# Strassen projections in 49 block products: two sets of PSUM banks, and x, bv and the result summed at the output by accumulating DMAs

## The chip, the core and the metric

The kernel runs on one NeuronCore of one Trainium2 chip. A core has TensorE (PE, with its weight loads as PEld), VectorE (DVE), ScalarE (ACT), GpSimd (POOL) and SyncE (SP), which here only issues DMAs; 16 DMA engines serve their queues. Each engine works through its own instructions in order and waits on semaphores for the others. The metric is device time in microseconds. Times are those of single executions and their median; the profile is of one more execution.

## What is computed

The input x has 128 batches of 128 rows (nodes) by 512 columns. All is float32. Cut to what matters:

```
h  = relu(layernorm(x))                       # layer 0
A  = adj @ h                                  # 128 x 512 per batch
x1 = x + relu(max_n A + b0)                   # one number c per row of each batch
h  = relu(layernorm(x1)); q, k, v = h @ Wq + bq, h @ Wk + bk, h @ Wv + bv
w  = softmax(q k^T / 8 + mask(adj))           # 8 heads of 64 columns
out = x1 + w v
```

The kernel uses that adding c to a whole row changes nothing in the layernorm after it (but for eps), so one normalised h serves both layers; and that the mask can be a product with 0 or 1 after the exponential. bv is added to the end result, since the weights sum to 1. Sums of weights that leave a safe range would send the program to a plain second path (`general`), which does not run with these inputs.

## The kernel before, in words

Batches are taken in 32 groups of four (G = 4); a group is processed in a pipeline, while the projections of q and k are made for the next group and the normalisation for the one after it. The three projections are matrix products of 512 x 512 (4 batches x 128 rows against 512 columns, over 512), done by the Strassen-Winograd scheme: the operands are cut into halves in both directions, and seven products of halves, p1 to p7, take the place of eight. A second level cuts five of the seven (p2, p3, p4, p5, p7) once more into seven products of quarters, each one 128x128x128 matmul, while p1 and p6 stay as four matmuls of 256 columns. So a projection has 8 matmuls of 256 columns (L483) and 35 of 128 (L596). In the first group (q, k and v) and for the last group's v the five are not cut.

The operands of such products are sums. `h_sum` (L381) makes sums of halves of the transposed h (t1 to t4), `h_blocks` (L398, on POOL) the sums of quarters; `weight_sums` and `weight_blocks` do the same for the weights, once, at the start. The products are combined in PSUM where signs allow, and else outside: terms that enter several results are kept in scratch banks, and DVE adds them to U, T7 and the results (L648, L674, L527, L536), POOL adds T7 to U (L699), ACT copies with the bias (L498). PSUM has eight banks of 512 columns; a bank that is written again must have been read before.

In each group, in PE's order: `apply` of the group before (64 matmuls L795; DVE divides by the sums, L812 and L813), `scores` (32 matmuls, L765; ACT exponentiates, L773), then v of this group, q and k of the next. In between stand one matmul for the adjacency of a batch (`product`, L350; DVE takes its maximum, L354), the layernorm (DVE L286 and L287, ACT L300 and L301, POOL's small operations, `norm_end` on ACT, L310), and the transpose of h: DVE transposes 32x32 blocks (`blocks`, L323), and 16 DMAs of SP put them in place (`move`, L333). POOL multiplies the weights by the mask (L777), adds bv to x (L316) and x to the result (L825); ACT adds c to x (L821); SP stores one batch at a time (L826).

The order is written out by hand (`manual_schedule`): each engine has its instructions in the order in which the Python code issues them, with no scheduler. `steps`, `later` and the table `next_norms` say after which product which other work is issued. Tiles come from pools with a set number of buffers: x has 7 (pairs of batches), most sums have one.

Of the kernel before, what the change touches and what calls it, by code (L numbers as in the profile page):

```python
# [52 lines left out]
P = 128  # L53
G = 4
# [115 lines left out]
def tile_adj_preln_d2(  # L170
# [16 lines left out]
    T = G * D  # L187
    HT2 = T // 2

# [3 lines left out]
    WS = {n: const.tile([P, 4, 2, N // 2], F32, name=f"s{n}_sb") for n in "qkv"}  # L193

    WB = {
        n: const.tile([P, 4 if n == "v" else 3, 4, P], F32, name=f"ss{n}_sb") for n in "qkv"
    }
# [5 lines left out]
    mhalf = const.tile([P, 1], F32, name="mhalf")  # L203
# [3 lines left out]
    db_sb = const.tile([P, 2, 2], F32, name="db_sb")  # L207
    DB = {n: db_sb[:, i] for i, n in enumerate("qk")}
    ones = const.tile([P, 1], F32, name="ones")
    flag = const.tile([1, 1], I32, name="flag")  # L210
    V = const.tile([P, G, H, HE], F32, name="v")
    U = const.tile([P, 3, 2, N // 2], F32, name="u")
    T7 = const.tile([P, 2, N // 2], F32, name="t7")

    def fast(ctx):
        xpool = ctx.enter_context(tc.tile_pool(name="xpool", bufs=7))
# [7 lines left out]
        X, HN, TB, HT, HB, H2, QT, KT, C, AMAX, WA, RSTD, NMR, PR = ({} for _ in range(14))  # L224
# [26 lines left out]
        nc.scalar.activation(live[:, 0:1], mhalf, AF.Copy)  # L251
# [7 lines left out]
        for p in range(2, 5):  # L259
            load(p)  # L260
# [3 lines left out]
        nc.gpsimd.memset(V[:, :, :, HD:HE], 1.0)  # L264
# [6 lines left out]
        def norm(m):  # L271

            g, i = divmod(m, G)
            if i == 0:
                HT[g] = proj.tile([P, G, NC, D], F32, name="hT")
                AMAX[g] = stat.tile([P, G], F32, name="amax")
                C[g] = stat.tile([P, G], F32, name="c")
            if m < G:
                if m == 0:
                    O[0] = one.tile([P, G, N], F32, name="o")  # L280
                HN[m] = O[0][:, m]
            else:
                HN[m] = work.tile([P, N], F32, name="hn", bufs=3)
            st = stat.tile([P, 6], F32, name="st")
            mv = stat.tile([P, 2], F32, name="mv")
            nc.vector.bn_stats(st, x_of(m))  # L286
            nc.vector.bn_aggr(mv, st)  # L287
            ve = stat.tile([P, 1], F32, name="ve")
            nc.vector.tensor_scalar_add(ve, mv[:, 1:2], EPS)
            rstd = RSTD[m] = stat.tile([P, 1], F32, name="rstd")  # L290
            nc.gpsimd.tensor_tensor(rstd, ve, mhalf, op=ALU.pow)
            nmr = NMR[m] = stat.tile([P, 1], F32, name="nmr")
            nc.gpsimd.tensor_scalar(nmr, mv[:, 0:1], rstd, -1.0, op0=ALU.mult, op1=ALU.mult)

        def norm_act(m):

            HN[m] = work.tile([P, N], F32, name="hn", bufs=3)
            neg = stat.tile([P, 1], F32, name="neg", bufs=2)
            sq = stat.tile([P, 1], F32, name="sq", bufs=2)
            nc.scalar.activation(HN[m], x_of(m), AF.Copy, scale=-1.0 / N, accum_out=neg)  # L300
            nc.scalar.activation(HN[m], x_of(m), AF.Square, bias=neg, accum_out=sq)  # L301
            ve = stat.tile([P, 1], F32, name="ve")
            nc.gpsimd.tensor_scalar(ve, sq, 1.0 / N, EPS, op0=ALU.mult, op1=ALU.add)
            rstd = RSTD[m] = stat.tile([P, 1], F32, name="rstd")
            nc.gpsimd.tensor_tensor(rstd, ve, mhalf, op=ALU.pow)
            nmr = NMR[m] = stat.tile([P, 1], F32, name="nmr")
            nc.gpsimd.tensor_tensor(nmr, neg, rstd, op=ALU.mult)  # L307

        def norm_end(m, bv=True):
            nc.scalar.activation(HN[m], x_of(m), AF.Relu, scale=RSTD[m], bias=NMR[m])  # L310
            if m >= G and bv:
                add_bv(m)

        def add_bv(m):
            x_m = x_of(m)
            nc.gpsimd.tensor_tensor(x_m, x_m, bv_sb, op=ALU.add)  # L316
# [28 lines left out]
        PA = {}  # L345

        def product(m):

            PA[m] = bank(7 if m >= G else 5 + m % 2)
            nc.tensor.matmul(PA[m], adjT, HN[m], start=True, stop=True)  # L350

# [10 lines left out]
        def h_quarters(g):  # L362
            if g in HB:
                return
            t = HT[g]

            t1 = t[:, 2:4, 0:2]
            if g == 0:
                t1 = one.tile([P, 4, D], F32, name="h23").rearrange("p (t c) d -> p t c d", t=2)
            HB[g] = dict(  # L370
                t1=t1,
                b11=t[:, 0:2, 0:2], b12=t[:, 2:4, 0:2], b21=t[:, 0:2, 2:4], b22=t[:, 2:4, 2:4]
            )

        def h_sum(g, k, eng=nc.vector):

            o, a, b = ("t3 b22 b12", "t1 b12 b11", "t2 b22 t1", "t4 b21 t2")[k].split()
            h_quarters(g)
            if o != "t1":
                HB[g][o] = one.tile([P, 2, 2, D], F32, name=f"hs{k}")  # L380
            eng.tensor_tensor(HB[g][o], HB[g][a], HB[g][b], op=ALU.subtract)  # L381

        def h_blocks(g, k, parts=range(3)):

            h_quarters(g)
            b = HB[g]["t4 b22 b21 t1 t3".split()[k]].rearrange("p t c d -> p c t d")
            if 0 in parts:
                H2[g, k] = one.tile([P, 4, D], F32, name=f"h2{k}")
            t = H2[g, k]

            sums = (
                (t[:, 0:2], b[:, :, 1], b[:, 0]),
                (t[:, 2], b[:, 1, 1], t[:, 0]),
                (t[:, 3], b[:, 1, 0], t[:, 2]),
            )
            for i in parts:
                o, x, y = sums[i]
                nc.gpsimd.tensor_tensor(o, x, y, op=ALU.subtract)  # L398

        def w_blocks(n, k):  # L400

            if k < 3:
                return [WB[n][:, k, e] for e in range(4)]
            if k == 3:
                a = WA[n]["a21"]
                return [a[:, e // 2, e % 2 * P : (e % 2 + 1) * P] for e in range(4)]
            if n == "v":
                return [WB[n][:, 3, e] for e in range(4)]
            return [WA[n][a][:, 0, P : 2 * P] for a in "a22 s4 a12 s1".split()]

        def weight_blocks(eng, n, ks=(3, 2, 0, 1, 4)):

            for k in ks:
                a = WA[n]["a22 s4 a12 s1 s3".split()[k]].rearrange("p c (o f) -> p o c f", o=2)
                s = w_blocks(n, k)
                for o, x, op, y in (
                    (s[0], a[:, 1, 0], ALU.add, a[:, 1, 1]),
                    (s[2], s[0], ALU.subtract, a[:, 0, 0]),  # L420
                    (s[1], a[:, 0, 0], ALU.subtract, a[:, 1, 0]),
                    (s[3], a[:, 0, 1], ALU.subtract, s[2]),
                ):
                    eng.tensor_tensor(o, x, y, op=op)

        def weight_sum(eng, n, k):

            if k == 0:
                w = W[n]
                WA[n] = dict(  # L430
                    a11=w[:, 0:2, 0:HT2], a21=w[:, 0:2, HT2:N],
                    a12=w[:, 2:4, 0:HT2], a22=w[:, 2:4, HT2:N],
                    **{f"s{j + 1}": WS[n][:, j] for j in range(4)},
                )
            o, a, op, b = ("s1 a21 + a22", "s2 s1 - a11", "s3 a11 - a21", "s4 a12 - s2")[k].split()
            eng.tensor_tensor(  # L436
                WA[n][o], WA[n][a], WA[n][b], op=ALU.add if op == "+" else ALU.subtract
            )
# [5 lines left out]
        class Products:  # L444

            def __init__(self, g, n):
                self.g, self.n = g, n
                self.run, self.five = {}, {}
                self.k0 = 3 if n == "q" else 0
                if n == "q":
                    QT[g] = one.tile([P, NC, T], F32, name="qT")
                elif n == "k":
                    KT[g] = one.tile([P, NC, T], F32, name="kT")  # L460
                o_t = "(o d) -> p {} o t d" if n == "v" else "(t d) -> p {} o t d"
                r = "t" if n == "v" else "o"
                self.bk = lambda x: x.rearrange(f"p {r} " + o_t.format(""), d=D)

            def dst(self, f, t):

                if self.n == "v":
                    return V[:, 2 * t : 2 * t + 2, 4 * f : 4 * f + 4, 0:HD]
                o = (QT if self.n == "q" else KT)[self.g]
                return o[:, 2 * f : 2 * f + 2, t * HT2 : (t + 1) * HT2]  # L470

            def view(self, ap):
                return ap.rearrange("p r (h d) -> p r h d", d=HD) if self.n == "v" else ap

            def mm(self, bank, a, b, first=False, parts=range(4)):
                a, b = WA[self.n][a], HB[self.g][b]
                for i in parts:
                    r, c = divmod(i, 2)
                    if self.n == "v":
                        lhs, rhs = b[:, r, c], a[:, c]  # L480
                    else:
# [552 lines left out]
```

## Time and profile before

| what | value |
|---|---|
| median of 3 runs | 1491.02 us (1489.36 to 1491.72) |
| span of the profiled execution | 1491.1 us |
| granted TensorE clock, mean | 0.998 |
| time from a group's scores to the next one's | 45.66 us |
| matmul records | 14565 |
| DMA share of 16 engines | 27.3% on SP's queue, 105.66 MB in all |
| POOL's queue for DMAs | 176 packets, 0.27 MB (four small loads at the start) |

The profiled execution's own time is its span: from the first to the last instruction it is 1491.1 us, and the median of the runs is the same within 0.1 us. How to read the lines that follow: in a timeline the first number is the start in us from the span's start, the second the length; then engine, source line, operation, output and inputs by name, output shape, how many instructions are merged. In brackets stands the engine's idle time just before, and what ended it. Each float32 matmul leaves two records in the trace, so counts of PE records are about twice those of matmuls. Lengths of instructions that follow each other overlap by some hundredths of a microsecond, so the cost to an engine is better read from start to start.

### The profile page before, as it was taken

The numbers are of one execution on the slowest core, as the hardware profiler recorded it, in microseconds if no ns is written. First come the engines' busy times: TensorE is split into PE (matmuls) and PEld (weight loads), VectorE is DVE, ScalarE is ACT, GpSimd is POOL, SyncE is SP. The second block draws the span as 40 slices with busy tenths as digits, with TensorE's granted clock in tenths as the row PEclk, the third lists the DMA queues.
The fourth block names the chain that finished last, engine by engine and source line by source line (L and its number), as shares of the span: only waits on it lengthen the run. The fifth ranks groups of instructions, "written<-read, shape, count | busy, mean of one in ns | idle before, by whom it ended". The sixth has DMA issues, their size and how long they took to land.

```text
span 1491.1 us, 38559 instructions
## 1 busy us (share of the span) xinstructions
PE 1467.8 (98%) x14565; PEld 1336.0 (90%) x14565; DVE 1170.0 (78%) x2909; ACT 680.0 (46%) x1550; POOL 1326.0 (89%) x1578
## 2 busy tenths in 40 slices
PE   8999999999999999999999999999999999999997
PEld 6899989999999999899999999999999989999997
DVE  7787877778877778777787777787777877778877
ACT  3444454454454444544544544445444444444442
POOL 7989989899899898898998989989999989899882
PEclk9999999999999999999999999999999999999999
DMA  4232222331223322233222233122332222331211
GB/s 167 55 86 52 54 77 77 86 74 38 77 75 83 86 41 65 76 78 86 60 52 74 76 85 86 29 76 76 79 86 55 54 75 76 86 86 26 63 43 59
DMA packets 307835, 105.66 MB, mean 71 GB/s; under 512 B 273152, under 2 KB 273280, under 8 KB 307648
## 3 DMA queue, kind: packets, MB, share of 16 engines
q1 hardware_dynamic: 307328, 102.84, 27.3%
q8 instruction: 117, 1.92, 0.5%
q14 instruction: 70, 0.57, 0.1%
q0 software_dynamic: 176, 0.27, 0.1%
q10 hardware_dynamic: 144, 0.07, 0.0%
HBM read 37.03 MB, written 33.55 MB: 47 GB/s over the span
## 4 chain that ended last, share of the span: by engine, by line
PE 67%; POOL 26%; DVE 3%; SPq 1%; issue 1%; DMA 1%; ACT 0%; DVEq 0%; POOLq 0%
PE bk L596 30%; POOL h L398 17%; PE bk L483 16%; PE bk L795 8%; PE bk L765 8%; POOL u L699 7%; PE bk L350 5%; POOL hs L381 2%; SPq L333 1%; DVE u L674 1%; DMA wk_sb<-in_L_gnn_Wk_dram 1%; DVE hs L381 0%; DVE sk_sb L436 0%; DMA hT<-tb 0%; DVE o L813 0%
## 5 line engine op out<-in xcount | busy, mean ns | idle before, releaser
L777 POOL TENSOR_TENSOR w<-w,live 128x512 f32<-128x512 f32 x248 | 308.5, 1277 | 0.0
L699 POOL TENSOR_TENSOR u<-u,t 128x512 f32<-128x512 f32 x184 | 235.0, 1277 | 74.1 <-DVE t L648 50.2
L674 DVE TENSOR_TENSOR u<-u,bk 128x256 f32<-128x256 f32 x552 | 206.3, 414 | 65.1 <-POOL u L699 39.0
L773 ACT ACTIVATE w<-bk 128x512 f32<-128x512 f32 x256 | 128.9, 624 | 270.4 <-PE bk L765 270.4
L648 DVE TENSOR_TENSOR u<-u,bk 128x128 f32<-128x128 f32 x368 | 109.2, 317 | 101.3 <-PE bk L596 99.4
L825 POOL TENSOR_TENSOR o<-xp,o 128x512 f32<-128x512 f32 x122 | 152.1, 1283 | 20.1 <-DVE RS L812 20.1
L310 ACT ACTIVATE hn<-xp,nmr,rstd 128x512 f32<-128x512 f32 x124 | 100.7, 812 | 142.9 <-POOL nmr L307 98.1
L316 POOL TENSOR_TENSOR xp<-xp,bv_sb 128x512 f32<-128x512 f32 x128 | 159.2, 1276 | 0.7 <-issue 0.7
L354 DVE TENSOR_REDUCE amax<-bk 128x1 f32<-128x512 f32 x128 | 86.6, 677 | 79.1 <-PE bk L350 79.1
L795 PE MATMUL bk<-v,w 128*64 128x65 f32 x4096 | 128.5, 223 | 0.0
L795 PEld LDWEIGHTS bk<-v,w 128*64 128x64 f32 x4096 | 124.0, 138 | 4.1 <-issue 0.3
L350 PE MATMUL bk<-hn,adjT 128*128 128x512 f32 x248 | 126.9, 593 | 0.0
L498 ACT ACTIVATE u<-bk,bq_sb 128x256 f32<-128x256 f32 x124 | 52.6, 480 | 160.2 <-PE bk L483 160.2
L765 PE MATMUL bk<-qT,kT 64*128 64x128 f32 x2048 | 122.9, 275 | 0.0
L765 PEld LDWEIGHTS bk<-qT,kT 64*128 64x128 f32 x2048 | 116.8, 188 | 2.5 <-issue 0.3
L596 PE MATMUL bk<-ssv_sb,h 128*128 128x128 f32 x720 | 111.7, 277 | 0.1
L596 PEld LDWEIGHTS bk<-ssv_sb,h 128*128 128x128 f32 x720 | 98.8, 191 | 14.2 <-issue 13.9
L398 POOL TENSOR_TENSOR h<-hT,h 128x128 f32<-128x128 f32 x186 | 96.8, 521 | 7.3
L596 PEld LDWEIGHTS bk<-h,ssq_sb 128*128 128x128 f32 x558 | 77.0, 191 | 26.9 <-DVE u L674 19.3
L813 DVE TENSOR_TENSOR o<-bk,RS 128x448 f32<-128x448 f32 (+1 forms) x161 | 93.7, 582 | 5.5
L596 PE MATMUL bk<-h,ssq_sb 128*128 128x128 f32 x558 | 91.0, 281 | 6.5 <-DVE u L674 6.4
L821 ACT ACTIVATE xp<-xp,c 128x512 f32<-128x512 f32 x128 | 91.3, 715 | 0.0
(201 smaller groups left out, 4080.2 us busy)
## 6 DMA issues: line engine op xcount, KB each, us to landing
out_dram<-o SPq DMA_DIRECT2D x128, 256.0 KB, 2.5
xp<-in_x_dram SPq DMA_DIRECT2D x62, 512.0 KB, 5.0
hT<-tb SPq DMA_DIRECT2D x992, 32.0 KB, 2.0
xp<-in_x_dram SPq DMA_DIRECT2D x4, 256.0 KB, 4.3
wq_sb<-in_L_gnn_Wq_dram SPq DMA_DIRECT2D x2, 512.0 KB, 8.3
wk_sb<-in_L_gnn_Wk_dram SPq DMA_DIRECT2D x2, 512.0 KB, 10.4
wv_sb<-in_L_gnn_Wv_dram SPq DMA_DIRECT2D x2, 512.0 KB, 11.4
bv_sb<-in_L_gnn_bv_dram POOLq DMA_DIRECT2D x1, 256.0 KB, 7.5
```

What stands on the lines that cost most here:

```text
L316: nc.gpsimd.tensor_tensor(x_m, x_m, bv_sb, op=ALU.add)
L350: nc.tensor.matmul(PA[m], adjT, HN[m], start=True, stop=True)
L398: nc.gpsimd.tensor_tensor(o, x, y, op=ALU.subtract)
L483: nc.tensor.matmul(bank[:, r, :], lhs, rhs, start=first and i == 0, stop=i == 3, skip_group_check=True,)
L596: nc.tensor.matmul(out, lhs, rhs, start=start, stop=True, skip_group_check=True)
L674: nc.vector.tensor_tensor(to, to, what, op=ALU.add)
L699: nc.gpsimd.tensor_tensor(u, u, T7, op=ALU.add)
L765: nc.tensor.matmul(psc[j][:, f, :], KT[g][r, f, i * D : (i + 1) * D], QT[g][r, f, i * D : (i + 1) * D], start=True, stop=True,)
L773: nc.scalar.activation(w[:, j], psc[j], AF.Exp, scale=HD ** -0.5)
L777: eng.tensor_tensor(w[:, j], w[:, j], live_h, op=ALU.mult)
L795: nc.tensor.matmul(pav[r, c : c + HE], w[:, h % 2, h // 2, r], V[:, i, h, :], start=True, stop=True,)
L825: eng.tensor_tensor(y, x_of(b), y, op=ALU.add)
```

## The change

All seven products of halves are now cut into seven products of quarters: a steady projection has 49 matmuls of 128 columns. They are no longer combined term by term. Each projection is made of two sets, S and D. S holds, for each product of halves, four of its seven block products side by side in one bank (512 columns), D the other three (384 columns). Within a set the seven products of halves are combined as a plain Strassen-Winograd step, in three banks (S in 0 to 2, D in 3 to 5): ACT copies, DVE adds a bank and an SBUF tile. The S results go to the place of q, k or v itself, the D results to a scratch tile `ud`. At the end the quarters are put together by sums in SBUF: `inner`, four sums that combine quarters of S, and `both`, which adds D. For v they run on POOL, for q on DVE, for k on both, one half each.

```diff
+        class Set:
+            def products(self, p):
...
+                if self.kind == "S":
+                    todo = ((0, "a00", "b00"), (3, "s0", "t0"), (2, "s1", "t1"), (1, "s2", "t2"))
+                else:
+                    todo = ((0, "a01", "b10"), (1, "s3", "b11"), (2, "a11", "t3"))
...
+                    nc.tensor.matmul(
+                        bk[:, k * P : (k + 1) * P], lhs, rhs,
+                        start=p in (1, 6, 5) and i == 0, stop=True, skip_group_check=True,
+                    )
...
+            def add(self, to, bank, what):
+                nc.vector.tensor_tensor(to, self.src(bank), what, op=ALU.add)
+
+            def step(self, p):
+                self.products(p)
...
+                elif p == 7:
+                    self.add(t(1, 1), self.b, t(1, 0))
+                    self.add(t(1, 1), self.c, t(1, 1))
+                elif p == 4:
+                    self.add(t(1, 0), self.b, t(1, 0))
+                elif p == 3:
+                    self.add(t(0, 1), self.c, t(0, 1))
+
+            def inner(self, k, eng, ts=None):
+                d = whole(self.n, self.g)
+                o, x_ = (d[:, :, i] for i in ((1, 0), (2, 1), (1, 3), (3, 2))[k])
...
+                eng.tensor_tensor(o, o, x_, op=ALU.add)
+
+            def both(self, eng, ts=None):
...
+                eng.tensor_tensor(d, d, u, op=ALU.add)
```

A set's order on PE is 1, 6, then 4 and 3 of the set before, then 5, 2, 7 (`sequence`). `h_blocks` makes the blocks of p1 and p2 in one tile A, of p5 and p3 in one tile B, and those of 6, 7 and 4 apart; all four `h_sum` run on DVE. What is issued after which step is in one table; steps are named by projection, set and product:

```diff
+        MASKS = "vS1 vS1 vS1 vS1 qD3 kS5 kS2 kS7".split()
+        TASKS = {
+            "vS1": lambda g, m: nxt(g, (stats, (m, m + 1)), (small, (m, m + 1))),
+            "vS6": lambda g, m: [(h_sum, g + 1, 5)] + nxt(g, (norm_end, m)),
...
+            "vS2": lambda g, m: [(h_blocks, g + 1, "A", (0, 2))] + nxt(g, (norm_act, m + 2)),
+            "vD6": lambda g, m: [(h_sum, g + 1, 6), (h_blocks, g + 1, "6")],
+            "vS3": lambda g, m: [(h_blocks, g + 1, "B", (0, 2))] + nxt(g, (norm_act, m + 3)),
...
+            "vD7": lambda g, m: [(h_sum, g + 1, 7), (h_blocks, g + 1, "7")],
+            "vD4": lambda g, m: [(h_sum, g + 1, 4), (h_blocks, g + 1, "4")],
...
+            "qS3": lambda g, m: own(g, (inner, "v", 3, PL), (both, "v", PL)) +
+                [(inner, "q", k, DV) for k in range(2)],
+            "qD5": lambda g, m: nxt(g, (blocks, m + 3), (move, m + 3)),
+            "qD7": lambda g, m: [(inner, "q", k, DV) for k in (2, 3)],
+            "qD3": lambda g, m: [(both, "q", DV, 0)],
+            "kD6": lambda g, m: [(both, "q", DV, 1)],
+            "kS3": lambda g, m: [(inner, "k", k, PL, 1) for k in range(4)] + [(inner, "k", k, DV, 0) for k in range(2)],
+            "kD7": lambda g, m: nxt(g, (product, m + 2)) + [(inner, "k", k, DV, 0) for k in (2, 3)],
+            "kD4": lambda g, m: [(both, "k", DV, 0)],
+            "kD3": lambda g, m: [(both, "k", PL, 1)] + nxt(g, (maximum, m + 2)),
+        }
```

The scores of a group use the banks in another order (3, 4, 5, 0, 1, 2, 6, 7), and the last batch's exponentials are issued after the first v product, then four adds of c. The output is summed in memory instead of in SBUF: SP copies x to the output, DRAM to DRAM; POOL issues a DMA that adds bv to it, and one that adds the result, to which ACT has added c. The adds of bv to x and of x to the result on POOL are gone, and x's pool has 3 buffers instead of 7.

```diff
+        def add_c(b):
+            y = O[b // G][:, b % G]
+            nc.scalar.activation(y, y, AF.Identity, bias=C[b // G][:, b % G : b % G + 1])
...
+        def start_out(g):
+            nc.sync.dma_start(rows(out, g), rows(x, g))
+
+        def out_bv(g):
+            nc.gpsimd.dma_start(
+                rows(out, g), bv_sb.unsqueeze(1).to_broadcast([P, G, N]), accum_op=ALU.add
+            )
+
+        def out_y(g):
+            nc.gpsimd.dma_start(rows(out, g), O[g], accum_op=ALU.add)
...
+                        for i, s in enumerate(("vS1", "vS1", "vS6", "vS6")):
+                            add(s, add_c, b - G + i)
+                        add("vS7", adjacency, m - 1)
...
+                    add("vD7", start_out, g)
+                    add("kD1", out_bv, g)
```

The first group's k and v stay uncut (`Level`), its q plain; the last group's v is now cut, with its final sums half on DVE and half on POOL. The weights have more sums of quarters, made at the start and in the first group. The two layernorm batches of a pair share their small POOL operations.

## The prediction

> **What bounds the kernel now.** I read the page's first part first, then one steady group in the timeline, engine by engine. A group is four batches; the score matmuls come back every 45.66 us (starts at 91.72 and 137.38), 32 times in a span of 1491.1 us, which is within 0.1 us of the median of the runs, so span and time are taken as one. The page:
>
> ```profile
> PE 1467.8 (98%) x14565; PEld 1336.0 (90%) x14565; DVE 1170.0 (78%) x2909; ACT 680.0 (46%) x1550; POOL 1326.0 (89%) x1578
> ```
>
> Busy PE alone proves little, since matmuls overlap; the starts do. PE's timeline (start, length, line, count; each matmul leaves two records):
>
> ```profile
> 714.87 0.71 PE L596 MATMUL bk<-h,ssq_sb 128*128 128x128 f32 x4 [0.20 <-DVE u L674]
> 715.42 1.89 PE L483 MATMUL bk<-hT,wk_sb 128*128 128x256 f32 x8
> 717.15 0.38 PE L596 MATMUL bk<-h,wk_sb 128*128 128x128 f32 x2
> 717.37 0.39 PE L596 MATMUL bk<-hT,sk_sb 128*128 128x128 f32 x2
> ```
>
> The reader sees starts without gaps: four 256-column matmuls take 1.73 us (0.433 each), a 128-column one 0.2235. The only wait in this group is 0.20 us. So PE's own rate bounds the steady groups. A group is 64 applies (3.94), 32 scores (3.77), 4 adjacency products (3.46), 24 x 0.433 = 10.39 and 105 x 0.2235 = 23.47: 45.03 of 45.66.
>
> Next I asked how near the others are. POOL is busy 41.6 us of that group, DVE 36.1, ACT 21.4 (the windows view, 700.50 to 746.17). POOL is second by little. Then I looked for the two working on SBUF at once, because the change adds to that. In the first 26 us, DVE's timeline and then POOL's:
>
> ```profile
> 17.31 0.68 DVE L436 TENSOR_TENSOR sk_sb<-wk_sb 128x512 f32<-128x512 f32 x1
> 17.91 1.75 DVE L436 TENSOR_TENSOR sk_sb<-wk_sb,sk_sb 128x512 f32<-128x512 f32 x1
> 19.59 1.75 DVE L381 TENSOR_TENSOR hs<-hT 128x512 f32<-128x512 f32 x1
> 21.26 1.75 DVE L381 TENSOR_TENSOR h<-hT 128x512 f32<-128x512 f32 x1
> ```
>
> ```profile
> 17.77 1.35 POOL L436 TENSOR_TENSOR sv_sb<-wv_sb 128x512 f32<-128x512 f32 x1 [0.92 <-DMA wv_sb<-in_L_gnn_Wv_dram]
> 19.19 1.59 POOL L436 TENSOR_TENSOR sv_sb<-sv_sb,wv_sb 128x512 f32<-128x512 f32 x1
> 20.75 1.71 POOL L436 TENSOR_TENSOR sv_sb<-wv_sb 128x512 f32<-128x512 f32 x1
> ```
>
> The same 128x512 DVE operation with both inputs in SBUF takes 0.68 us while POOL rests and 1.75 beside a running POOL operation; POOL's go from 1.27 (its usual) to 1.71. Each DVE operation ends about 0.5 us after a POOL one: they take turns. In steady groups the kernel before has only two such DVE operations:
>
> ```profile
> 702.18 0.83 DVE L381 TENSOR_TENSOR hT<-hT 128x512 f32<-128x512 f32 x1
> 703.93 0.68 DVE L381 TENSOR_TENSOR hs<-hT 128x512 f32<-128x512 f32 x1
> ```
>
> ```profile
> 702.54 0.79 POOL L398 TENSOR_TENSOR h<-hs,h 128x128 f32<-128x128 f32 x1
> 704.09 0.83 POOL L398 TENSOR_TENSOR h<-hT,h 128x128 f32<-128x128 f32 x1
> ```
>
> There a 128x128 POOL operation grows from 0.46 to 0.8. DVE operations with one input in PSUM show no such growth (L536: 0.68 beside POOL).
>
> **PE.** In every steady projection 8 matmuls of 256 columns become 14 of 128: 8 x 0.433 - 14 x 0.2235 = 0.335 us less, 1.0 us a group, over 92 projections 31 us. The last v, plain before (28 x 0.433), becomes 49 x 0.2235: 1.2 us less. A group's PE work is then 44.1 us. A rule speaks against this: the Trainium skill, "TensorE: Matmul & The Clock Gate", section "Back-to-back issue gap", gives a sustained spacing of 81 ns at 128 columns and 131 ns at 512, naming no type; weights then cost so much that halving the width saves little. Put on a line, 256 columns would cost 98 ns, and 42 narrow matmuls instead of 24 wide would cost 45% more instead of 10% less: +4.7 us a group. The row here has 0.2235 against 0.433, nearly proportional, and I follow the row.
>
> **ACT.** Copies of sets replace the activations, and the c-add moves to the new y. About 24 us a group against 21.4: no bound. But its order matters. After the scores it runs in order six exps (L773 row: 4.03 us for 8), the first v copy, two exps, four c-adds (0.62 each), two norm ends (0.70), a v copy, a norm_act (1.47) and only then the copy of v's first D product. From the first exp at 5.1 us into the group that copy is done near 17, though its matmuls end near 14. Behind it on DVE stand the sixth D add and h_sum 6; behind those POOL's blocks of 6, B, A3 and 7. POOL rests about 3.6 us, and the blocks of 7 come about 1 us after PE wants them. Cost 0 to 1.6 us a group; I take 1.
>
> **POOL.** Gone: bv-adds, residuals and T7 adds (4 + 4 + 6 operations of about 1.24 us, 17), two h_sums (2.5). Kept: eight masks (9.9). Blocks of h become 15 operations (11.0 by the L398 rows: 0.42, 0.68 and 1.24 start to start, with the waits between dependent ones). New: v's inner adds 4 x 1.24, v's D add of 1,536 elements (3.5, on the line through 0.68 at 256 and 1.24 at 512), half of k's (3.0 + 1.9), small operations 2.6, and two DMA issues. No accumulating DMA is in the trace; the nearest rows are POOL's four issues at the start, 0.55 to 0.79 us each. I take 0.8 and, since 512 rows of 2 KB are new, 3 as the upper end; nothing excludes a cost, none can be a gain. Sum 38.5, and with the rest of 3.6: 42 without DVE's interference.
>
> **DVE.** Gone: the scattered adds of runs and fives (L648, L674). New per group: 15 evacuations of 512 (0.61 start to start) and 15 of 384 (0.48, between 0.34 and 0.61); with apply (3.65), statistics (1.8), maxima (2.4) and transposes (2.5) 26.8 us. Then 15 operations with both inputs in SBUF where 2 were: four h_sums, q's four inner adds and two D adds, k's four half inner adds and one D add: 8.9 us alone. Total 35.7, as before, if POOL leaves them alone. It doesn't: POOL works nearly all the time, and 14 of the 15 fall where it does (h_sum 6 falls in its rest). What each waits is bounded by the rows: 0.28 (a 128x128 DVE operation beside POOL's took 0.54 for 0.26) and 1.0 (the 512s above); v's D add of 3.5 us could hold one longer. Most stand beside POOL's 1.24 us operations, some in pairs: I take 0.65, 9.1 us a group, ends 3.9 and 14. The Trainium skill, "SBUF — State Buffer", section "Who interferes with whom", says that a DVE instruction with two SBUF inputs contends with a GpSimd (POOL) instruction that reads SBUF, for one shared port held for a whole instruction. By the full-lock rule a random arrival beside 1.24 us waits 0.62; the rows have 1.0 for those in a row. My 0.65 stands between.
>
> DVE cannot use its free time for this: from the scores to the sixth D add it waits for PE and ACT, about 6 us (1.2 after the statistics, 1 before the seventh adds, 2.7 before the sixth D add, the rest in pieces). The late part, from q's inner adds to the last maximum, has no gap: in it a wait goes straight to the evacuations of k, which are queued behind q's and k's sums, and PE stops at the seventh and fourth product of k, whose banks must be read first. Sum: 35.7 + 9.1 + 6 = 50.8 us a group, against PE's 44.1 + 1. POOL's loss (0.44 per 512, less for smaller) is some 5 us: 47, hidden under that.
>
> **DMA.** The trace has 27% of the engines. A copy of x to the output and two additions of 1 MB are added per group. h's moves have some 9 us of slack, now issued earlier; x has three buffers, each free most of a group before its next load; SP issues 16 moves at 0.65 us. I cost them at nothing in steady groups: start, bv and y have 20 to 30 us each between issue and need. If one took that long, apply would wait for o.
>
> **Ends.** In the first group POOL has 13.8 us of weight sums beside its work: +3, ends 0 and 6. At the tail the last c-adds and one 1 MB addition replace four 256 KB stores (2.5 us): by the 512 KB load's 5.0 and bv's 7.5 us, +5, ends 2 and 10. The last v gains 1.2 and waits for its sums: 0.
>
> **Sum.** 29 groups x (50.8 - 45.66) = +149; ends +8; 1491 + 157 = 1648, rounded to 1645.
>
> **Rivals.** (1) PE still bounds: DVE's waits stay below about 1 us a group in the late part, because the sums fall between POOL's operations. It is the one case on the other side, and decides at that point: 44.3 us a group, -39 + 8, so 1460. For it: both engines alone have room. Against it: every L381 and L436 row above. (2) Mild contention, 3 to 5 us of waits: POOL or the blocks of 7 bound, 46 to 48.5 us, 1510 to 1580. (3) The additions bind POOL: at 3 us an issue POOL's 47 becomes 51.4 and k's last sum comes after the scores want it: 1665. That would show as POOL issue time, not long DVE operations. (4) More than 54 us, long locks under v's D add: over 1740. That the products aren't narrower is excluded: the changed program has 7,929 matmuls for 7,356.
>
> **Numbers.** Slower by contention, (3) included, 1580 to 1750: 60%. Mild: 16%. Over 1750: 8%. Faster: 12%. Within 0.2%, about what a measurement tells from no change: 4%, where ACT's and POOL's delays eat PE's gain. The range 1488 to 1750 leaves out 20%.
>
> **What would show it.** Right: q's inner adds on DVE (0.61 alone) at 1 us or more, the D adds at 1.5 or more, POOL's inner adds near 1.7, PE waiting for DVE before k's seventh, fourth and third products, and a group near 51 us. Wrong: these DVE rows at their lengths alone, or PE waiting for POOL's h blocks or ACT's copies; POOL's DMA issues at 3 us would move the cause to (3).

## The result and the profile after

| | before | after |
|---|---|---|
| median, us | 1491.31 (1489.36 to 1491.72, 4 runs) | 1669.47 (1666.41 to 1670.89, 4 runs) |
| ratio, with its 95% interval | | 1.1191 (1.1175 to 1.1207) |
| span of the profiled execution | 1491.1 | 1669.1 |
| to the first scores | 44.98 | 44.74 |
| first group, scores to scores | 46.74 | 54.59 |
| 30 groups after it | 1370.70 | 1530.81 |
| from the last scores to the end | 28.6 | 38.9 |

The change makes the kernel 178 us slower; the forecast was 1645. In the table the loss is 160 us in the 30 groups, 7.9 in the first, 10.3 at the end and -0.2 at the start. Most groups now take 50.70 us (before 45.66); nine of them take 51 to 53.

The first part of the page of the changed kernel (called after from here on), and its chain of work that ended last:

```profile
PE 1507.3 (90%) x15711; PEld 1394.1 (84%) x15711; DVE 1383.4 (83%) x2154; ACT 666.3 (40%) x1553; POOL 1314.1 (79%) x1377
```

```profile
DVE 34%; PE 26%; ACT 13%; POOL 13%; issue 12%; SPq 1%; DMA 1%; POOLq 0%; DVEq 0%; ACTq 0%
```

PE has more records than before and a lower share: it waits. DVE is at the head of the chain though it is busy 83% only; as before, the shares prove little. The windows view of one steady group, from one start of apply's divisions to the next (columns: length, then busy us of PE, PEld, DVE, ACT and POOL with their instructions, granted clock, DMA share, GB/s):

```profile
658.69:709.39 50.70, 45.75 (x496) 42.29 (x494) 43.24 (x69) 20.87 (x49) 40.77 (x43) 1.00 0.53 105
```

DVE's timeline in that group, around q's and k's sums, and then POOL's (the count x2 means two instructions in one row; the 768s are the D adds):

```profile
686.86 2.20 DVE L704 TENSOR_TENSOR qT<-qT 128x512 f32<-128x512 f32 x2
...
690.63 4.96 DVE L704 TENSOR_TENSOR qT<-qT 128x512 f32<-128x512 f32 x2
...
697.04 1.72 DVE L719 TENSOR_TENSOR qT<-qT,ud 128x768 f32<-128x768 f32 x1
...
700.47 1.47 DVE L719 TENSOR_TENSOR qT<-qT,ud 128x768 f32<-128x768 f32 x1
```

```profile
684.49 1.36 POOL L832 DMA_DIRECT2D out_dram<-o  x1
685.38 5.99 POOL L704 TENSOR_TENSOR v<-v 128x512 f32<-128x512 f32 x4
691.45 3.59 POOL L719 TENSOR_TENSOR v<-v,ud 128x1536 f32<-128x1536 f32 x1
695.01 4.88 POOL L773 TENSOR_TENSOR w<-w,live 128x512 f32<-128x512 f32 x3
```

The second pair of q's sums takes 4.96 us where two take 1.41 undisturbed (shown below). Cut out of the pair, its second sum starts at 691.95 and lasts 3.64: it begins after POOL's long D add of v (691.45 to 695.04) and ends 0.55 after it. Behind it on DVE stand k's evacuations, and PE waits for those; PE's timeline shows where:

```profile
690.18 0.49 PE L651 MATMUL bk<-hs,wq_sb 128*128 128x128 f32 x2 [0.28 <-DVE ud L668]
...
696.25 0.49 PE L651 MATMUL bk<-hs,sk_sb 128*128 128x128 f32 x2 [2.68 <-DVE kT L668]
...
699.42 0.49 PE L651 MATMUL bk<-hs,wk_sb 128*128 128x128 f32 x2 [0.67 <-DVE kT L668]
...
704.86 0.49 PE L651 MATMUL bk<-hs,wk_sb 128*128 128x128 f32 x2 [0.52 <-DVE ud L668]
```

The first wait stands before q's fourth product of D. The others stand before k's seventh product of S (2.68) and its fourth of S (0.67) and of D (0.52). The forecast named the seventh, the fourth and the third; before a third product PE does not wait in this group.

### The profile page after: what moved, and what is told of

It is laid out like the page before. It is cut to its first block, busy times and chain, and to the rows that moved or that the text cites. A ratio compares the mean times of both kernels' runs of the same rounds, so it can differ in the third digit from the quotient of the medians.

```text
span 1669.1 us, 39386 instructions
## 1 busy us (share of the span) xinstructions
PE 1507.3 (90%) x15711; PEld 1394.1 (84%) x15711; DVE 1383.4 (83%) x2154; ACT 666.3 (40%) x1553; POOL 1314.1 (79%) x1377
## 4 chain that ended last, share of the span: by engine, by line
DVE 34%; PE 26%; ACT 13%; POOL 13%; issue 12%; SPq 1%; DMA 1%; POOLq 0%; DVEq 0%; ACTq 0%
PE bk L651 12%; DVE ud L668 9%; PE bk L759 7%; DVE qT L704 7%; DVE kT L704 5%; ACT o L817 4%; DVE kT L668 4%; PE bk L792 3%; POOL h L438 3%; ACT hn L340 2%; POOL hB L438 2%; DVE qT L668 2%; DVE qT L719 2%; DVE amax L376 2%; PE bk L372 2%
## 5 line engine op out<-in xcount | busy, mean ns | idle before, releaser
L668 DVE TENSOR_TENSOR ud<-bk,ud 128x384 f32<-128x384 f32 x465 | 251.9, 547 | 103.0 <-ACT ud L659 69.0
L704 DVE TENSOR_TENSOR qT<-qT 128x512 f32<-128x512 f32 x124 | 214.9, 1733 | 3.2
L659 ACT COPY ud<-bk 128x384 f32<-128x384 f32 x186 | 88.4, 475 | 311.6 <-PE bk L651 310.4
L668 DVE TENSOR_TENSOR v<-bk,v 128x512 f32<-128x512 f32 x155 | 103.9, 687 | 107.3 <-PE bk L651 106.2
L704 POOL TENSOR_TENSOR v<-v 128x512 f32<-128x512 f32 (+1 forms) x124 | 175.7, 1417 | 8.9 <-DVE v L668 1.7
L438 POOL TENSOR_TENSOR h<-hs 128x256 f32<-128x256 f32 x93 | 68.3, 735 | 98.8 <-DVE hs L414 98.8
L704 POOL TENSOR_TENSOR kT<-kT 128x256 f32<-128x256 f32 x124 | 98.6, 795 | 33.9 <-DVE kT L668 26.6
L668 DVE TENSOR_TENSOR qT<-bk,qT 128x512 f32<-128x512 f32 x155 | 104.5, 686 | 20.1 <-PE bk L651 19.1
L719 POOL TENSOR_TENSOR kT<-kT,ud 128x768 f32<-128x768 f32 x31 | 56.2, 1814 | 71.9 <-DVE ud L668 70.3
L719 POOL TENSOR_TENSOR v<-v,ud 128x1536 f32<-128x1536 f32 x30 | 107.6, 3588 | 2.4
L668 DVE TENSOR_TENSOR kT<-bk,kT 128x512 f32<-128x512 f32 x155 | 103.0, 679 | 1.5 <-PE bk L651 0.4
```

The lines of the kernel that those rows point to most:

```text
L438: eng.tensor_tensor(h[:, :, 0:2], b[:, :, :, 1], b[:, :, 0], op=ALU.subtract)
L668: nc.vector.tensor_tensor(to, self.src(bank), what, op=ALU.add)
L704: eng.tensor_tensor(o, o, x_, op=ALU.add)
L719: eng.tensor_tensor(d, d, u, op=ALU.add)
```

## The experiments

Theory 1: DVE's sums with two inputs in SBUF and POOL's operations take turns, which makes DVE late. The rivals: (2) ACT's late copy of v's first D product, (3) the accumulating DMAs, (4) DVE has too much work even undisturbed. Medians are in us; each ratio is to the kernel before on the same chip.

**One input in place of two.** Each sum of q and of DVE's half of k became a transpose of the same tile; the sums are left out.

```diff
+                if eng is nc.vector and self.n != "v":
+                    eng.transpose(o, x_)
+                    return
                 eng.tensor_tensor(o, o, x_, op=ALU.add)
```

> The changed kernel with DVE's sums of q and of its half of k (L704, L719) each replaced by a 32x32-block transpose of the same tiles: as many DVE instructions of the same sizes, but with one SBUF input in place of two. These sums are left out. Theory 1 (a DVE operation with two SBUF inputs and POOL's operations take turns, which makes DVE the bound): the replaced operations take 0.6 to 0.9 us each instead of 1.1 to 2.5, POOL's inner adds of v fall from 1.5 to 1.25, the group falls from 50.7 to 45 to 47 us, the time to 1490 to 1555. Theory 4 (DVE has too much work even when nobody disturbs it): the same number of operations is left, so 1640 to 1675. Theory 3 (the accumulating DMAs, by POOL's issue time and the load on memory): unchanged, 1650 to 1675. Theory 2 (ACT's late copy makes POOL's blocks late): 1640 to 1675.

Measured 1506.75, ratio 1.0097 (1.008 to 1.0114), as theory 1 had it. The groups by line and form, of this kernel:

```profile
L705 DVE STREAM_TRANSPOSE qT<-qT 128x512 f32<-128x512 f32 x124 | 87.9, 709 | 3.2
L723 DVE STREAM_TRANSPOSE qT<-ud 128x768 f32<-128x768 f32 x62 | 59.8, 964 | 0.0
```

After has 1,733 ns and 1,489 ns for these two (L704 and L719, as many instructions). DVE keeps its number of instructions and their sizes, and 163 us go; theory 4 falls. Twelve of the 30 groups after the first take 45.1 us; the others take up to 49.2, which is taken up below.

**The sums left out.** The same places, with `return` alone.

> The changed kernel with DVE's sums of q and of its half of k left out altogether. Theory 1: the rest of DVE's work (some 28 us a group) is far from any bound, so the same as or up to 30 us under the kernel with one-input operations: 1470 to 1530, and the difference between the two is what these operations cost by their own length where they stand before k's evacuations. Theory 4: far below the one-input kernel, by 5 us a group or more (1480 to 1520 against 1640). Theory 3: 1620 to 1675, since the DMAs are all there. Theory 2: 1620 to 1675.

Measured 1508.36 (ratio 1.0107, 1.0086 to 1.0128), the same as with one-input operations. PE bounds in both, so here the length of these operations costs nothing; what costs is the turn-taking.

**POOL's sums of v left out.**

```diff
+                if eng is nc.gpsimd and self.n == "v":
+                    return
```

> The changed kernel with POOL's sums of v (four inner adds and the 1,536-element D add of each group, some 9.6 us of POOL beside DVE) left out; DVE does all that it did. Theory 1: q's inner adds, which stand beside these, fall from 2.2 and 4.95 us a pair to 1.4 to 2.2 a pair, and the group by 2.5 to 4.5 us though POOL is not the bound: 1530 to 1600. Theory 4: DVE's work is unchanged, 1650 to 1675. Theory 3: POOL keeps its two DMA issues; if they bound POOL, the group falls by up to POOL's 9.6 us, down to 1400 to 1450, but q's adds keep their lengths. Theory 2: unchanged within 15 us, since the blocks come before these sums.

Measured 1651.00 (1.1067, 1.1049 to 1.1086): every theory but the fourth missed, mine by 50 us. DVE's timeline of this kernel (its first row cut so that the first sum stands alone), then POOL's:

```profile
682.04 4.52 DVE L706 TENSOR_TENSOR qT<-qT 128x512 f32<-128x512 f32 x1
...
688.86 1.41 DVE L706 TENSOR_TENSOR qT<-qT 128x512 f32<-128x512 f32 x2
```

```profile
680.56 5.44 POOL L777 TENSOR_TENSOR w<-w,live 128x512 f32<-128x512 f32 x4
685.46 1.81 POOL L831 DMA_DIRECT2D out_dram<-bv_sb  x1
```

With nothing ahead of them, POOL's four masks had moved up beside q's first sum. That sum did not get a turn between them: it ended at 686.56, 0.56 us after the last of them (686.00). The second pair, with POOL at rest, takes 1.41. So the sum that was held up moved, and the total hardly did. Theory 1 needed a run in which POOL really rests.

**POOL's sums of v and its masks left out.** DVE's and PE's work is whole, both additions stay.

> The changed kernel without POOL's sums of v and without POOL's products with the mask (both are left out), with DVE's and PE's work whole and both additions in place. In the run without POOL's sums of v alone, at 1651.0 us, the masks and an issue moved up beside q's first inner add, which took 4.5 us, while the later ones took 0.7. Theory 1: with nothing of POOL beside them q's sums take 0.7 and 0.95 us; DVE has some 6 us of waits a group less, and PE bounds again at 45.1 to 46.5 us: 1500 to 1545, as with one-input operations. If DVE's sums are long by themselves (theory 4), or if the additions carry the loss (theory 3): 1620 or more.

Measured 1497.05 (1.0045, 1.0028 to 1.0062), within 0.5% of before. Groups by line and form:

```profile
L706 DVE TENSOR_TENSOR qT<-qT 128x512 f32<-128x512 f32 x124 | 86.9, 701 | 3.2
L706 DVE TENSOR_TENSOR kT<-kT 128x256 f32<-128x256 f32 x124 | 86.0, 694 | 2.1
L723 DVE TENSOR_TENSOR qT<-qT,ud 128x768 f32<-128x768 f32 x62 | 58.9, 949 | 0.0
```

q's sums are at 701 and 949 ns, and the group takes 45.45 us. k's small sums still meet POOL's half of k and stay at 694 ns. The same DVE work thus costs 172 us more when POOL has its own to do. With the first run this shows theory 1 from both sides.

**The long D add of POOL cut in two.**

```diff
-own(g, (inner, "v", 3, PL), (both, "v", PL))
+own(g, (inner, "v", 3, PL), (both, "v", PL, 0), (both, "v", PL, 1))
```

> The changed kernel with POOL's D add of v (128x1536, 3.6 us) cut into two instructions of 768 elements; the work is the same. Theory 1 in its strict form (POOL holds the shared port for a whole instruction): q's third and fourth inner add, a pair of 4.95 us beside it, falls to 3.0 to 3.8 us, the group by 0.5 to 1.7 us, the time to 1615 to 1655. If the two engines share the port element by element in some ratio: the pair stays at 4.95 and the time within 8 us of the changed kernel's, perhaps longer by POOL's extra start.

Measured 1642.91 (1.1018, 1.0999 to 1.1036). POOL's work is the same, 30 instructions are added, and 27 us go. DVE's row that answers to the 4.96 of after:

```profile
679.78 3.42 DVE L704 TENSOR_TENSOR qT<-qT 128x512 f32<-128x512 f32 x2
```

The sum waited for a whole instruction of POOL, not for a share of its elements. The group still takes 49.75 us: POOL is now less held up there, and its masks and its half of k come to lie beside DVE's sums of k, which take 1,045 ns each for 719.

**ACT's order.** The c-adds behind the late copy.

```diff
-for i, s in enumerate(("vS1", "vS1", "vS6", "vS6")):
+for i, s in enumerate(("vD1", "vD1", "vS3", "vS3")):
```

> The changed kernel with ACT's four adds of c issued after v's first D product (two) and after v's third S step (two) instead of after the first two steps of v, so that they stand behind the copy of v's first D product. Theory 2 (that late copy delays the sixth D add, h_sum 6 and POOL's blocks): DVE's wait for this copy (2.35 us in a group) shrinks by 1.5 to 2.5 us and the group by 1 or more, 1610 to 1640. Theory 1: what is saved before v's D sums becomes rest elsewhere in part, since the late part of the group sets the pace: a gain of 0 to 1 us a group, 1638 to 1670.

Measured 1664.03 (1.1163, 1.1144 to 1.1181): 5 us less. DVE's wait for the copy in a group went from 2.35 to 2.15 only, and the group from 50.70 to 50.62. ACT's timeline of this kernel shows why the copy is hardly earlier:

```profile
668.12 1.52 ACT L340 ACTIVATE hn<-xp,nmr,rstd 128x512 f32<-128x512 f32 x2 [2.13 <-POOL nmr L306]
```

The end of the layernorm, which stands before the copy, now waits for POOL's factors, and POOL computes these behind four masks. So this run does not show what an earlier copy would bring. That the late copy is not the cause of the loss is shown by the one-input run: there DVE waits the same 2.35 us for it, and the undisturbed groups take 45.1 us.

**The output part alone, in the kernel before.** No adds of bv and x on POOL; the copy of x, both additions, c on the result.

```diff
-                            residual(b - G + i, nc.gpsimd)
...
+                        add((1, 2, 3, 4)[i], add_c, b - G + i)
+                    add(5 if g + 1 < NG else 4, out_y, g - 1)
+                add(2, start_out, g)
+                add(12 if g + 1 < NG else 5, out_bv, g)
```

> The kernel before with only the output part of the change: no adds of bv to x and of x to the result on POOL; SP copies x to the output, two accumulating DMAs of POOL add bv and the result, ACT adds c to the result. Theory 1 (the output part costs nothing in steady groups): PE still bounds at 45.7 us a group, plus 5 to 10 us at the tail: 1490 to 1505. Theory 3 (the accumulating DMAs carry a good part of the loss): 1530 or more, with PE or ACT waiting for something that waits for the DMAs, or with slower moves of h.

Measured 1549.56 (1.0388, 1.0371 to 1.0406): theory 3's side, and a miss of mine. The groups take 47 to 48.5 us, the end 38.4. The next run asked whether this is POOL's issue or the transfer.

**The same, with the result's addition issued after q's fifth step:** `add(10 ...)` for `add(5 ...)`.

> The kernel before with only the output part, as in the run at 1549.6 us, but POOL's issue of the addition of the result stands after q's fifth step and not among POOL's blocks of h. There PE waited 0.6 us a group for a block and 0.43 for DVE behind POOL. If the price of the output part is the place of its issue in POOL's queue (theory 1's reading: an issue holds POOL for about 1.3 us and nothing else is lost): the group falls from 47.0 to 45.7 to 46.2 us, the time to 1500 to 1525, with some 10 us left at the tail. If the additions themselves slow the kernel (theory 3: memory traffic, waits for landing): still 1540 to 1555.

Measured 1632.86 (1.0932, 1.0913 to 1.095), wrong by both. The two additions now leave POOL 0.84 us apart, and run together with SP's moves of h. SP's rows for the 32 moves of a group, in the kernel before (scores at 685.92), with the early addition (scores at 654.01), then here (scores at 636.48):

```profile
672.15 22.35 SPq L333 DMA_DIRECT2D hT<-tb  x32
```

```profile
640.31 24.93 SPq L331 DMA_DIRECT2D hT<-tb  x32
```

```profile
621.55 29.79 SPq L331 DMA_DIRECT2D hT<-tb  x32
```

Counted from the scores, the last move is issued by 8.6 us before, by 11.2 with the early addition, and by 14.9 here. The last move lands 2.0 us after its issue in all three, but those issued while both additions run land after up to 11.1 us and are issued up to 2.0 us apart instead of 0.65. POOL's sum of h waits for the last:

```profile
652.90 1.26 POOL L379 TENSOR_TENSOR hs<-hT 128x512 f32<-128x512 f32 x1 [3.78 <-PE bk L594]
```

The row names PE, but the sum starts 0.2 us after the last move has landed; behind it stands the T7 add, for which DVE waits 3.48 us, and PE 2.83 for DVE. So the additions are not free: they slow what shares the DMA engines. In the changed kernel the moves end 1.0 us before the scores (709.74 against 710.70) and are first needed at h's first sum, 6.5 us after them; there the delay is covered.

**The changed kernel without the copy and the additions:** the result is stored by one plain DMA of SP per group; x and bv are not added.

> The changed kernel complete in its products and sums, with the result stored by one plain DMA of SP per group: the copy of x and the two additions are left out. Theory 1: POOL has 2.6 us a group less, but the sums still take turns with it; the steady group falls by 0 to 1 us, the tail by 5 to 10 us: 1630 to 1662. Theory 3: a good part of the 178 us goes, 1600 or less.

Measured 1651.76 (1.1069, 1.1049 to 1.1086), as theory 1 had it. The copy and the additions, left out together, cost the changed kernel 18 us: 7.5 at the end (31.4 for 38.9), the rest in groups.

**One-input operations and the plain store together.** Both leave out what they did above.

> The changed kernel with one-input transposes in place of DVE's sums of q and k (as in the run at 1506.8 us), and the result stored by one plain DMA of SP per group: the copy of x to the output and the two additions are left out. If the groups of 46 to 49 us in that run, in which PE waits up to 2.2 us for nothing the profile shows, come from the additions' traffic (theory 3 in a small form): all groups take 45.1 us, those waits are gone, the tail falls by 5 to 10 us, 1470 to 1485. If they come from elsewhere (the longer program, its instruction loads): the irregular groups stay and only the tail falls, 1493 to 1503.

Measured 1480.64 (0.9919, 0.9902 to 0.9935), as expected if the additions make the long groups. The windows view of a group:

```profile
681.29:726.40 45.11, 44.53 (x498) 41.96 (x495) 36.79 (x69) 20.99 (x49) 35.76 (x40) 1.00 0.29 71
```

Here the groups after the first, but the last, take 45.1 to 45.2 us, and PE waits nowhere on "issue". With the copy and the additions (the first run) it did, 17 us in all, for instance:

```profile
236.81 4.24 PE L765 MATMUL bk<-qT,kT 64*128 64x128 f32 x43 [2.18 <-issue]
```

So the long groups come with the copy and the additions, and the trace of the first run points to one of them: all 16 of these pauses begin while an addition of bv is under way, and no copy runs in them. The additions need not cost this: in the run without POOL's sums of v and its masks both are in place, with that of bv issued 25 us after the scores instead of some 40. There PE never pauses on "issue", and the groups take 45.4 to 46.2 us. This run and the one before it differ only in the two-input sums: 171 us. It is 11 us under before, a bound on what the products and the rest of the schedule save when both costs are taken away; of the kernels that leave nothing out, none is faster than the one before.

**Added work in the kernel before.** On the output part alone (1549.6), 14 DVE operations of 128x512 a group to a scratch tile that nobody reads; first sums of two SBUF tiles, then transposes of one.

```diff
+            nc.vector.tensor_tensor(SCR, W["q"][:, 0, :], W["k"][:, 0, :], op=ALU.add)
...
+                    for s in (*range(6, 18), 11, 17):
+                        add(s, extra)
```

> The kernel before with the output part of the change (as in the run with that part alone, but six buffers of x) and 14 added DVE sums of 128x512 in each group, after the steps of q and k, from two SBUF tiles to a scratch tile that nobody reads. None of the 49 block products is in it. Theory 1: each takes 1.2 to 1.9 us beside POOL (0.68 alone), DVE has 36 + 14 x 1.5 = 57 us, and the group becomes 50 to 58 us: 1620 to 1850. Theory 4 (work, not interference): the same time as the run with 14 one-input operations, within 20 us.

> The same with 14 added DVE transposes of a 128x512 SBUF tile to the scratch tile in place of the sums: one SBUF input. Theory 1: 0.63 us each, DVE 36 + 8.8 = 45 us, just under PE's 45.7; with the evacuations behind them a little late, 1495 to 1580, and well under the run with two inputs. Theory 4: the same as that run.

Measured 1880.12 (1.2612, 1.2591 to 1.2634) and 1693.87 (1.1365, 1.1346 to 1.1384). The two kernels' rows of the added operations:

```profile
L861 DVE TENSOR_TENSOR scr<-wq_sb,wk_sb 128x512 f32<-128x512 f32 x434 | 492.4, 1135 | 3.2
```

```profile
L861 DVE STREAM_TRANSPOSE scr<-wq_sb 128x512 f32<-128x512 f32 x434 | 301.6, 695 | 3.2
```

The first is 30 us over theory 1's range. They differ by 0.44 us an operation, 6.2 us a group (58.03 and 51.80 typically) and 186 us in all: turn-taking again, in a kernel with 43 matmuls to a projection and not 49. But the one-input run, forecast at 1580 at most, is 144 us above its base: in the order of before, 8.7 us of harmless work (14 x 0.62, start to start) cost 4.8 us a group. DVE's free time lies in waits ahead of evacuations, and an operation put before an evacuation delays it; PE waits 1.75 us a group for one of them (L647). For that kernel theory 4 is half right.

## Why the prediction was right, and by how much its terms missed

**DVE's sum** was 35.7 + 9.1 + 6 = 50.8 us. The steady group has 50.70: 43.24 busy and 7.46 idle. The waits, from the rows against the undisturbed lengths (1.41 for a pair of 512, 0.95 for 768, 0.85 for a pair of 256): 0.79 and 3.55 for q's pairs, 1.29 for its D adds, 1.14 for k's inner sums, 0.43 for h's sums: 7.2. Own work is then 36.0. So the mechanism was right, and the total came so near by luck, as two errors cancelled: the waits were forecast 1.9 too long, the forced idle 1.5 too short. The mean of 0.65 for 14 waits was near (0.51), but not the picture of equal turns: 2.95 of the 7.2 is one sum under one long POOL instruction, which the forecast had mentioned and not counted. The full lock of the Trainium skill, "SBUF — State Buffer", section "Who interferes with whom", which the forecast weighed, fits that sum (3.64) and the cut add (3.42 a pair); the other sums wait 0 to 0.8 us, and with them 0.65 was a fair mean.

**PE.** The forecast saved 1.0 of 45.46 us (45.66 less its wait); 44.53 in the windows row of the run with one-input operations and the plain store is 0.93 saved. The row's 0.2235 at 128 columns held; the estimate of 4.7 us more from the Trainium skill's spacing did not.

**POOL** was 38.5 without interference; the one-input run has 38.11 in a steady group, and after 40.77, so it loses 2.7, not 5. An issue of an addition takes 1.3 us by its row and 0.9 to the next start, against 0.8 assumed. Rival (3), which put it at 3, is out.

**ACT.** PE waits 0.6 us a group for the blocks of 7 (1 assumed); moving the c-adds gained 5 us, with the copy hardly earlier.

**DMA** was costed at nothing in steady groups. This is the term that was missing: copy and additions cost 18 us, 7.5 of it at the end; 30 groups have a mean of 51.03 us with them and 50.55 without, 14 us. The additions did not land too late (after 9.0 to 9.2 us, far under the 20 us at hand); they showed as pauses of PE, 5.7 us in after, and in the order of before as late moves. What makes up the rest of the 14 us was not separated.

**Ends** were put at 8 and are 18. The first group lost 7.9 (3 assumed): with one-input operations and the plain store it takes 50.16 us, 3.4 more than before, and with the sums and the plain store 55.33, so the rest is turn-taking, which I had left out of this term. The tail lost 10.3 (5 assumed), 7.5 of it by the copy and the additions.

Together: 30 groups at 5.0 are 150 (149 forecast), irregular groups 10, ends 18. The cause was named rightly; of the 24 us missed, 10 are the irregular groups, 10 the ends, and the rest the steady groups' 1 and the rounding from 1648 to 1645.

## What to carry to other kernels

Before work is given to two engines because both have free time, count the operations that get in each other's way: a DVE sum with two SBUF inputs can be held until the POOL instruction beside it has ended, so it wants short POOL instructions beside it, one operand from PSUM, or POOL at rest. Taking work from POOL does not help where its next work moves up into the same place. An accumulating DMA of 1 MB costs little to issue (1.3 us), but for 9 us it slows other DMAs: small ones that an engine waits for, and loads of instructions.

## What was not expected of the hardware

In the run without POOL's sums of v, POOL's masks in a row gave a DVE sum no turn for 3.8 us (4.52 for 0.70), in each steady group. That is not so of any masks in a row: in after the same four masks let q's D add in behind the one under way (the row at 697.04: 1.72 us for 0.95; cut apart, the mask behind it takes 1.98 for 1.27), and POOL's inner adds of v let a sum in too (1.47). What decides it was not separated. In the first case the masks' records overlap by 0.55 us, in after by 0.04.

An addition of 1 MB keeps the 16 DMA engines busy for 8 us. The windows view of the kernel before with the output part, around one (issued at 644.11; the last columns are DMA share and GB/s; a share above 1 comes of counting a packet whole where it starts):

```profile
644.00:646.00 2.00, 2.00 (x21) 2.00 (x20) 1.71 (x6) 1.54 (x3) 1.97 (x3) 1.00 0.32 50
646.00:648.00 2.00, 2.00 (x15) 1.52 (x14) 1.97 (x5) 0.00 (x0) 1.64 (x2) 1.00 1.13 72
648.00:650.00 2.00, 2.00 (x20) 1.93 (x18) 2.00 (x5) 0.00 (x0) 2.00 (x3) 1.00 1.10 190
650.00:652.00 2.00, 2.00 (x68) 1.95 (x68) 1.97 (x6) 0.00 (x0) 2.00 (x2) 1.00 1.24 212
652.00:654.00 2.00, 2.00 (x70) 1.94 (x64) 1.93 (x6) 0.00 (x0) 1.34 (x2) 1.00 1.15 186
```

PE's pauses on "issue", up to 2.2 us, come only with the additions, and the packets in the traces point to late loads of PE's own instructions. Queue q8 (its kind is given as "instruction") brings 126 packets of 16 KB. In the first run each of the 16 pauses follows one of them that started while an addition of bv was under way, and ends 1.2 to 1.7 us after it landed: the pause at 234.63 to 236.81 has a packet from 234.52 to 235.40. Counted in PE's records, these packets start 60 to 123 records later than the same ones in the run without copy and additions; the others start at most 72 later.

After a pause of PE the granted clock can fall. Two groups of the run without POOL's sums of v, with the same pause of 3.33 us in each (columns as above, the clock behind POOL's):

```profile
856.57:907.35 50.78, 46.65 (x498) 43.78 (x495) 41.53 (x68) 20.98 (x49) 30.79 (x38) 0.97 0.54 105
907.35:956.47 49.12, 45.01 (x497) 42.14 (x494) 41.51 (x68) 20.97 (x49) 30.76 (x38) 1.00 0.55 107
```

In the first of them, matmuls came every 0.43 us instead of 0.2235 for 3.4 us, from 1.3 us after the pause on, and the group is 1.7 us longer. The Trainium skill, "TensorE: Matmul & The Clock Gate", section "Part 1: The HAM clock gate", tells of half rate after an idle window of about 3.4 us that runs free of the program; that the same pause costs in one group and not in the next agrees. The length does not: these pauses are shorter than such a window, and in after one of 2.67 us, ending at 746.93, is enough: the granted clock of its group is 0.97. The mean clock of after is 0.972, but DVE's lateness covers it: groups with a fallen clock and without both take 50.70.
